# x's features on the partitions in another order: three weights loaded whole, and the places of the first and last groups searched anew

## Chip, cores and metric

The kernel runs on one core of a Trainium2 chip. The metric is device time in microseconds of one execution; the kernel before takes 2419.2 us, the median of three runs.

## What is computed

Two layers over 128 graphs of 128 nodes with 512 features, all in float32, with one mask `adj` for all graphs:

```python
# layer 0: attention, 8 heads of 64
q, k, v = x @ Wq + bq, x @ Wk + bk, x @ Wv + bv
attn = softmax(q_h k_h^T / 8 + (1 - adj) * -1e9)
x = layernorm(x + (attn v) @ Wo + bo)
# layer 1: graph attention
h = x @ W
e = leaky_relu(h a1 [i] + h a2 [j], 0.2) * adj
x = layernorm(x + elu(softmax(e) h + beta * h))
```

## The kernel before

**Groups.** The 128 graphs are done in 64 groups of two. The products of a group with a weight (512 x 512 against 512 x 256) are made of 2 x 2 blocks with seven products instead of eight: `product(name, g, n)` (L274) is the n-th of them. The sums of blocks that this needs are made once for each weight (`weight_sum`, L211: four steps, in place in part), and for each group's x (`block_sum`, L241, on GpSimd). The results come out of PSUM partly through ScalarE (`take_part`, L321) and partly through VectorE (`add_block`, L371), and a product that reuses a part of PSUM waits for the one that was read there.

**x with features on the partitions.** The products of q, k and v need x with its features on the partitions. `load_blocks` (L82) reads a group's x in four transfers, one for each quarter `a` of the features: partition `a*32 + r` gets the tokens `32 b + r`. `turn_x` (L233) then turns 32 x 32 blocks on VectorE, one instruction for each graph of the group, so that partition `a*32 + c` holds the features `a*128 + m*32 + c`, m = 0..3. Wq, Wk and Wv must have their rows in the same order, so `load_turned` (L102) reads each in four transfers to 32 partitions, four rows of 2 KB to a partition:

```python
queue(a, two).dma_start(
    out=t[a * Q : (a + 1) * Q],
    in_=src[a * P : (a + 1) * P].rearrange("(m c) f -> c m f", c=Q),
)
```

For Wq two of the four, and for the first x blocks two of the four, are issued from ScalarE, everything else of this from SyncE. Wo and W of layer 1 (`load_weight`, L128) are loaded with one transfer each to 128 partitions; biases, the mask, beta and the rows of a come through GpSimd's queue (`load_later`, L156).

**Order.** Nothing is left to a scheduler: `rows(g)` (L650) and `last_rows(g)` (L725) list the steps of a group with places, `other` (L792) replaces the places for the groups 0 to 3 and the last ones, and further steps (`weight_sum`, `wa_column`, `make_beta`, the loads) get places of their own. `lay` adds 37.33 per group, and the steps are issued sorted by place; so a place says only what stands ahead of what on each engine, and each engine works through its list in order, waiting where data are missing.

```python
for place, (_, fn, *args) in zip(places, own):
    at(g * STEP + place, fn, *args)
```

At the start TensorE multiplies the identity 20 times (`keep_busy`, L141) while the first loads run. In the last group the seven products of Wo and W give way to plain ones (`plain`, L351), whose weights are loaded a second time into the tiles of Wq and Wk (`load_again`, L131).

Of the kernel before, what the change touches and what calls it, by code (L numbers as in the profile page):

```python
# [13 lines left out]
P = 128  # L14
Q = 32
# [3 lines left out]
STEP = 37.33  # L19
# [3 lines left out]
def gnn_two_layers(  # L23
# [34 lines left out]
    nc = tc.nc  # L58
# [19 lines left out]

    def queue(a, two):
        return nc.scalar if two and a >= 2 else nc.sync  # L80

    def load_blocks(g):  # L82
        t = grp.tile([P, G, 4, P], F32, tag="xb", name=f"xblk_{g}", bufs=1)
        for a in range(4):
            queue(a, g == 0).dma_start(
                out=t[a * Q : (a + 1) * Q].rearrange("r t b d -> r (t b) d"),
                in_=x[g * G : (g + 1) * G, :, a * P : (a + 1) * P].rearrange(
                    "t (b r) d -> r (t b) d", r=Q
                ),
            )  # L90
        return t
# [10 lines left out]
    def load_turned(t, src, two=False):  # L102
        for a in range(4):
            queue(a, two).dma_start(
                out=t[a * Q : (a + 1) * Q],
                in_=src[a * P : (a + 1) * P].rearrange("(m c) f -> c m f", c=Q),
            )
# [14 lines left out]
    load_turned(wq_sb, wq, two=True)  # L122
# [110 lines left out]
    def turn_x(g, t):  # L233
        if t == 0:
            xT[g] = grp.tile([P, NC, G * N], F32, tag="xT", name=f"xT_{g}")
        nc.vector.transpose(
            xT[g][:, :, t * N : (t + 1) * N].rearrange("p m (b r) -> p b m r", r=Q),
            xblk[g][:, t].rearrange("p b (m c) -> p b m c", c=Q),
        )
# [485 lines left out]
    def last_rows(g):  # L725
        b0, b1 = g * G, g * G + 1
        return (
            (-61.75, fetch_blocks, g), (-45.225, turn_x, g, 0), (-43.975, turn_x, g, 1),
            (-41.605, block_sum, "x", g, 3), (-40.445, block_sum, "x", g, 1),
            (-39.705, block_sum, "x", g, 2), (-38.965, block_sum, "x", g, 4),  # L730
            (-27.57, product, "k", g, 1), (-25.805, product, "q", g, 7),
            (-24.91, product, "k", g, 7), (-23.25, take_part, "k", g, 1, 0, 0),
            (-23.145, product, "q", g, 1), (-21.38, product, "k", g, 6),
            (-18.97, take_part, "k", g, 6, 1, 0), (-18.31, take_part, "q", g, 1, 0, 0),
            (-17.675, fetch_x, b1), (-17.225, fetch_x, b0), (-14.395, product, "q", g, 6),
            (-13.085, take_part, "q", g, 6, 1, 0), (-12.825, residual, b0),
            (-12.63, product, "k", g, 2), (-11.545, residual, b1),
            (-11.515, add_block, "k", g, 0, 0, 2, 1), (-10.865, product, "q", g, 5),
            (-9.75, take_part, "q", g, 5, 1, 1), (-7.98, product, "k", g, 5),
            (-7.97, add_block, "q", g, 1, 1, 7, 5), (-6.865, take_part, "k", g, 5, 1, 1),  # L740
            (-6.215, product, "q", g, 2), (-6.02, add_block, "k", g, 1, 1, 7, 5),
            (-5.32, product, "k", g, 4), (-4.425, product, "k", g, 3),
            (-4.355, add_block, "q", g, 0, 0, 2, 1), (-3.31, take_block, "k", g, 0, 1),
            (-1.79, product, "q", g, 4), (-0.575, add_block, "q", g, 1, 0, 4, 6),
            (-0.155, add_block, "k", g, 1, 0, 4, 6), (-0.025, product, "q", g, 3),
            (1.09, take_block, "q", g, 0, 1), (1.97, scores, b0), (3.09, scores, b1),
            (3.56, mask, b0, 0), (3.99, product, "v", g, 1), (4.23, mask, b0, 1),
            (4.9, row_max, b0), (5.08, take_part, "v", g, 1, 0, 0), (6.12, mask, b1, 0),
            (6.26, exps, b0, 0), (6.6, product, "v", g, 6), (7.05, exps, b0, 1),
            (7.24, mask, b1, 1), (7.84, exps, b0, 2), (7.91, row_max, b1), (8.63, exps, b0, 3),  # L750
            (9.21, product, "v", g, 2), (9.42, exps, b1, 0), (9.56, row_inv, b0),
            (10.21, normalise, b0, 0), (10.81, normalise, b0, 1),
            (10.82, add_block, "v", g, 0, 0, 2, 1), (11.4, product, "v", g, 7),
            (11.41, normalise, b0, 2), (12.01, normalise, b0, 3), (12.61, exps, b1, 1),
            (12.75, attn_write, b0), (13.78, exps, b1, 2), (14.57, exps, b1, 3),
            (15.9, attn_read, b0), (16.55, row_inv, b1), (16.66, take_part, "v", g, 6, 1, 0),
            (17.04, normalise, b1, 0), (17.64, normalise, b1, 1), (17.83, product, "v", g, 5),
            (18.62, normalise, b1, 2), (19.22, take_part, "v", g, 5, 1, 1),
            (19.6, normalise, b1, 3), (19.74, add_block, "v", g, 1, 1, 7, 5),
            (19.75, product, "v", g, 3), (20.34, attn_write, b1), (20.58, turn_attn, b0, 0),  # L760
            (20.62, product, "v", g, 4), (21.24, turn_attn, b0, 1),
            (21.36, take_block, "v", g, 0, 1), (22.6, add_block, "v", g, 1, 0, 4, 6),
            (23.49, attn_read, b1), (24.37, attend, b0), (26.17, attend_evict, b0),
            (26.99, plain, "w", b0), (27.96, turn_attn, b1, 0), (28.62, turn_attn, b1, 1),
            (30.8, plain_take, b0), (30.89, attend, b1), (32.15, attend_evict, b1),
            (32.83, row_product, b0, 0), (33.56, row_product, b0, 1), (33.6, plain, "w", b1),
            (34.29, bn_stats, y, b0, "c"), (35.87, bn_aggr, b0, "c"),
            (36.07, add_eps, g, "c", 0), (37.3, plain_take, b1), (37.51, inv_std, g, "c", 0),
            (37.96, bn_stats, y, b1, "c"), (38.65, bn_aggr, b1, "c"),
            (38.85, add_eps, g, "c", 1), (39.02, scale_s, g, 0), (39.16, inv_std, g, "c", 1),  # L770
            (39.66, spread_s2, g, 0), (39.95, row_product, b1, 0), (40.68, row_product, b1, 1),
            (41.41, scale_s, g, 1), (41.58, edge, g, 0), (41.72, spread_s2, g, 1),
            (41.91, leaky, g, 0), (42.18, edge_max, g, 0), (42.45, norm_c, b0),
            (42.59, edge_exp, g, 0), (42.79, keep_busy, 6, "late"), (42.98, edge, g, 1),
            (43.31, leaky, g, 1), (43.58, edge_max, g, 1), (43.99, edge_exp, g, 1),
            (44.27, edge_inv, g, 0), (44.44, weights, g, 0), (44.77, edge_inv, g, 1),
            (44.94, weights, g, 1), (45.27, norm_c, b1), (45.83, turn_weights, g, 1),
            (46.03, turn_weights, g, 0), (46.25, weights_evict, g, 1),
            (46.55, weights_evict, g, 0), (46.69, aggregate, b1), (47.61, aggregate, b0),
            (48.34, aggregate_evict, b1), (48.93, aggregate_evict, b0), (49.07, plain, "h", b1),  # L780
            (52.52, plain, "h", b0), (53.85, elu_exp, b1), (55.81, elu_max, b1),
            (56.19, elu_exp, b0), (56.5, elu_sum, b1), (57.19, elu_max, b0),
            (57.88, elu_sum, b0), (58.57, bn_stats, u, b0, "f"), (59.26, bn_aggr, b0, "f"),
            (59.46, add_eps, g, "f", 0), (59.63, bn_stats, u, b1, "f"),
            (59.77, inv_std, g, "f", 0), (60.32, bn_aggr, b1, "f"), (60.52, add_eps, g, "f", 1),
            (60.69, shift, g, 0), (60.83, inv_std, g, "f", 1), (61.03, norm_f, b0),
            (61.71, shift, g, 1), (61.95, store, b0), (62.05, norm_f, b1), (62.97, store, b1),
        )
# [5 lines left out]
            1.72, 6.92, 7.58, 8.38, 15.14, 9.12, 15.88, 9.52, 11.53, 12.205, 10.415, 14.215,  # L794
            13.1, 17.525, 16.63, 18.64, 15.37, 11.31, 17.745, 13.995, 19.45, 16.52, 18.555,
            20.565, 15.79, 15.82, 21.365, 19.67, 21.375, 20.47, 20.48, 22.49, 21.595, 22.27,
            23.165, 24.28, 27.92, 24.7, 29.2, 25.825, 26.945, 27.18, 27.85, 14.89, 28.52, 15.76,
            16.85, 29.74, 29.88, 30.41, 33.58, 30.67, 31.46, 32.25, 17.37, 33.38, 33.72, 24.955,
            34.32, 28.715, 26.045, 35.73, 36.33, 34.94, 37.07, 36.93, 37.72, 27.845, 38.51,
            40.22, 28.935, 39.44, 40.62, 41.22, 34.8, 41.82, 42.42, 43.16, 46.31, 44.24, 44.9,  # L800
            50.26, 34.035, 43.68, 50.92, 35.8, 36.96, 46.57, 52.35, 48.57, 53.22, 54.23, 54.09,
# [194 lines left out]
```

## Time and profile before

| | |
|---|---|
| median of three runs | 2419.2 us (2416.99 to 2421.52) |
| the profiled execution | 2418.33 us, span 2416.6 us |
| granted TensorE clock, mean | 0.998 |
| busy share: TensorE, VectorE, ScalarE, GpSimd | 99%, 79%, 62%, 36% |
| data moved | 245.30 MB, 102 GB/s over the span |
| Wk: four transfers of 256 KB | 9.4 us from issue to landing, median |
| Wo: one transfer of 1024 KB | 7.6 us from issue to landing |
| first x blocks to use | VectorE starts to turn them at 5.17 us |

Spans and idle times are of one profiled execution, in microseconds from its start. A group of instructions is named by line, engine, operation and what it writes and reads. `pq`, `pk`, `pv` are PSUM tiles of the products for q, k, v (`eq`, `ev` the second ones), `tx` the block sums of x, `s_q`, `s_k`, `s_v` those of the weights, `psc` the scores, `po` the attention's output.

### The profile page before, as it was taken

Reading aid. Unit: us, or ns where it says so; the run is one execution under the profiler, and the core shown is the slowest. Engines: PE = TensorE matmul, PEld = TensorE weight load, DVE = VectorE, ACT = ScalarE, POOL = GpSimd, SP = SyncE. Lnnn points to the kernel's source line nnn. Section 1 sums busy time; section 2 is a strip of 40 time slices with the busy share of each in tenths; the row PEclk is TensorE's granted clock in tenths of the full one; section 3 lists DMA queues with packets and bytes.
Section 4 is the critical chain, followed back from the end, with each engine's and each line's share of the span. In section 5 each row is a group of like instructions: output and inputs, shape, how many; then the busy total and the mean of one; then the engine's idle time right before and its main releaser. Section 6 shows DMA issues by size and latency. Waiting matters only on the chain. (4 is left out here: it accounts for less than half of the span.)

```text
span 2416.6 us, 50056 instructions
## 1 busy us (share of the span) xinstructions
PE 2390.7 (99%) x17956; PEld 2206.0 (91%) x17956; DVE 1910.6 (79%) x4385; ACT 1487.9 (62%) x5310; POOL 860.6 (36%) x1045
## 2 busy tenths in 40 slices
PE   8999999999999999999999999999999999999998
PEld 7899999999999999999999999999999999999985
DVE  5777887788787877877877878778778787787787
ACT  3565666656656666566566566665665666656655
POOL 5332333324323333333233233332342333323332
PEclk9999999999999999999999999999999999999999
DMA  6323334334243243342342432423423324334331
GB/s 179 106 79 106 108 79 122 94 91 123 76 110 115 78 115 95 90 123 79 106 118 76 114 105 80 123 93 92 122 77 109 110 80 118 96 88 123 88 106 70
DMA packets 202633, 245.30 MB, mean 102 GB/s; under 512 B 18881, under 2 KB 149953, under 8 KB 202385
## 3 DMA queue, kind: packets, MB, share of 16 engines
q1 hardware_dynamic: 201152, 240.46, 34.7%
q8 instruction: 142, 2.33, 0.4%
q0 software_dynamic: 400, 0.86, 0.2%
q14 instruction: 107, 0.87, 0.1%
q10 hardware_dynamic: 832, 0.79, 0.1%
HBM read 141.37 MB, written 100.66 MB: 100 GB/s over the span
## 5 line engine op out<-in xcount | busy, mean ns | idle before, releaser
L411 ACT ACTIVATE s<-s,nmax 128x128 f32<-128x128 f32 x1024 | 397.7, 394 | 4.9 <-DVE nmax L405 4.8
L425 ACT ACTIVATE sb<-s,rinv 128x128 f32<-128x128 f32 x1024 | 327.0, 392 | 25.7 <-DVE rinv L418 20.3
L256 POOL TENSOR_TENSOR tw<-oT 128x256 f32<-128x256 f32 x63 | 46.2, 733 | 768.0 <-DVE oT L474 768.0
L445 POOL TENSOR_TENSOR x<-x,bo_b_in 128x512 f32<-128x512 f32 x128 | 164.3, 1294 | 362.4 <-DMA x<-in_x_dram 361.9
L317 ACT ACTIVATE part_q<-pq,bq_c 128x128 f32<-128x128 f32 x384 | 119.0, 361 | 239.0 <-PE pq L303 238.8
L411 ACT ACTIVATION_READ_ACCUMULATOR s<-s,nmax 128x1 f32 x1024 | 196.7, 192 | 0.0
L317 ACT ACTIVATE part_k<-pk,bk_c 128x128 f32<-128x128 f32 x384 | 120.2, 364 | 116.6 <-PE pk L303 69.4
L589 ACT COPY attT<-pat 128x256 f32<-128x256 f32 (+1 forms) x65 | 23.9, 369 | 263.0 <-PE pat L586 263.0
L397 DVE SCALAR_TENSOR_TENSOR s<-psc,amask 128x512 f32<-128x512 f32 x256 | 164.6, 683 | 25.7 <-PE psc L389 25.7
L454 DVE STREAM_TRANSPOSE attnT<-ab 128x512 f32<-128x512 f32 x256 | 178.8, 701 | 4.2 <-DMA ab<-scr 4.1
L514 DVE SCALAR_TENSOR_TENSOR ya<-w,wa_row 128x512 f32<-128x512 f32 x256 | 174.2, 681 | 4.4
L405 DVE TENSOR_REDUCE nmax<-s 128x8 f32<-128x1024 f32 x128 | 156.1, 1220 | 4.3
L327 DVE TENSOR_TENSOR part_w<-pw,x 128x256 f32<-128x256 f32 x189 | 80.0, 424 | 85.1 <-PE pw L297 85.0
L303 PE MATMUL pk<-xT,wk_sb 128*128 128x128 f32 x1024 | 139.8, 280 | 1.8 <-DMA wk_sb<-in_L_gnn_Wk_dram 1.8
L303 PE MATMUL pq<-xT,wq_sb 128*128 128x128 f32 x1024 | 135.1, 275 | 1.6 <-DMA wq_sb<-in_L_gnn_Wq_dram 1.4
L303 PEld LDWEIGHTS pq<-xT,wq_sb 128*128 128x128 f32 x1024 | 129.4, 192 | 5.5 <-issue 1.6
L303 PEld LDWEIGHTS pk<-xT,wk_sb 128*128 128x128 f32 x1024 | 129.0, 191 | 6.0 <-issue 1.9
L389 PE MATMUL psc<-kT,qT 64*128 64x128 f32 x2048 | 132.0, 279 | 0.0
L313 ACT COPY part_v<-pv 128x256 f32<-128x256 f32 x192 | 70.0, 365 | 100.3 <-PE pv L297 100.3
L389 PEld LDWEIGHTS psc<-kT,qT 64*128 64x128 f32 x2048 | 119.4, 188 | 11.7 <-issue 11.4
L464 PE MATMUL po<-attnT,v 128*64 128x128 f32 x2048 | 127.0, 276 | 1.3 <-DVE attnT L454 1.3
L599 PEld LDWEIGHTS pz<-attT,x 128*128 128x128 f32 x1024 | 124.3, 192 | 4.1 <-ACT attT L589 0.5
(681 smaller groups left out, 6544.0 us busy)
## 6 DMA issues: line engine op xcount, KB each, us to landing
scr<-sb SPq DMA_DIRECT2D x128, 512.0 KB, 2.7
ab<-scr SPq DMA_DIRECT2D x512, 128.0 KB, 3.1
x<-in_x_dram SPq DMA_DIRECT2D x128, 256.0 KB, 5.0
out_dram<-u SPq DMA_DIRECT2D x128, 256.0 KB, 2.1
xblk<-in_x_dram SPq DMA_DIRECT2D x254, 128.0 KB, 5.5
wk_sb<-in_L_gnn_Wk_dram SPq DMA_DIRECT2D x4, 256.0 KB, 9.4
wv_sb<-in_L_gnn_Wv_dram SPq DMA_DIRECT2D x4, 256.0 KB, 11.1
wo_sb<-in_L_gnn_Wo_dram SPq DMA_DIRECT2D x1, 1024.0 KB, 7.6
```

The lines of the kernel that those rows point to most:

```text
L303: nc.tensor.matmul(out[:, m * N : (m + 1) * N], a[:, c, m * P : (m + 1) * P], b[:, c, :], start=first and m == 0 and c == 0, stop=(c == 1) ...
L317: nc.scalar.activation(dst[:, m, :], src[:, m * N : (m + 1) * N], AF.Identity, bias=col)
L389: nc.tensor.matmul(psc[b][j][:, m, :], qT[g][feats, m, rows], kT[g][feats, m, rows], start=True, stop=True,)
L397: nc.vector.scalar_tensor_tensor(s_t[b][:, j * HP : (j + 1) * HP, :], psc[b][j], SCALE, amask.rearrange("p (o n) -> p o n", o=1).broadcast ...
L405: nc.vector.tensor_reduce(nmax[b], s_t[b], AX.X, ALU.max, negate=True)
L411: nc.scalar.activation(s_t[b][:, h, :], s_t[b][:, h, :], AF.Exp, bias=nmax[b][:, h : h + 1], accum_out=rsum[b][:, h : h + 1],)
L425: nc.scalar.mul(sb[b][:, :, h, :], s_t[b][:, h, :].rearrange("p (b c) -> p b c", c=Q), rinv[b][:, h : h + 1],)
L445: nc.gpsimd.tensor_tensor(xr[b], xr[b], later["bo"], ALU.add)
L454: nc.vector.transpose(attnT[b].rearrange("p h (a r) -> p a h r", r=Q)[:, rows], ab[b].rearrange("p a (h c) -> p a h c", c=Q)[:, rows],)
L464: nc.tensor.matmul(po[b][j * HD : (j + 1) * HD, m, :], vb[b][:, h * HD : (h + 1) * HD], attnT[b][:, j * HP + m, :], start=True, stop=True,)
L514: nc.vector.scalar_tensor_tensor(z, y[b], 1.0, wa_row[j], ALU.mult, ALU.mult, accum_out=s12[g][:, i, j : j + 1])
L599: nc.tensor.matmul(pz[b][:, c, :], x1[b][:, c * P : (c + 1) * P], attT[g][:, i, :], start=True, stop=True,)
```

## The change

The feature order is now `a*128 + 4 c + m` on partition `a*32 + c`. Four neighbouring rows of a weight then belong to one partition, and partition p has the rows 4p to 4p + 3, which lie together in memory (8 KB); each of Wq, Wk and Wv is one transfer to 128 partitions, from SyncE. `turn_x` reads the x blocks with a step of four elements. No other step changes what it does.

The places are new for the groups 0, 1 and 2, for the later part of group 3, for the last four groups and for the steps outside the groups. At the start of TensorE's list the order is now q1, q2, q7, v1, v2, q6, k1, k2, q5, k7, k6, q4, k5, q3, k3, k4, then k1 of group 1 and the scores of group 0; before it was q1, q2, q7, k1, k2, k7, v1, v2, k6, q6, k5, q5, k3, q3, q4, k4, q1 of group 1, v6, scores. SyncE now issues x of group 0 and W of layer 1 ahead of the x blocks of group 1, and Wo after them. On VectorE `make_beta` stands behind the first k add instead of behind the turn of group 1, and the first `wa_column` ahead of that turn. In the last group the two graphs change places in the second layer.

```diff
     def load_blocks(g):
...
-            queue(a, g == 0).dma_start(
+            (nc.scalar if g == 0 and a >= 2 else nc.sync).dma_start(
...
-    def load_turned(t, src, two=False):
-        for a in range(4):
-            queue(a, two).dma_start(
-                out=t[a * Q : (a + 1) * Q],
-                in_=src[a * P : (a + 1) * P].rearrange("(m c) f -> c m f", c=Q),
-            )
+    def load_turned(t, src):
+        nc.sync.dma_start(out=t, in_=src.rearrange("(p m) f -> p m f", m=NC))
...
-    load_turned(wq_sb, wq, two=True)
+    load_turned(wq_sb, wq)
...
-            xblk[g][:, t].rearrange("p b (m c) -> p b m c", c=Q),
+            xblk[g][:, t].rearrange("p b (c m) -> p b m c", c=Q),
...
-    at(16.62, load_later)
-    at(17.22, load_weight, wo_sb, wo)
-    at(19.82, load_weight, w1_sb, w1)
+    at(15.205, load_weight, w1_sb, w1)
+    at(15.265, load_later)
+    at(21.105, load_weight, wo_sb, wo)
...
-    at(20.89, make_beta)
+    at(19.425, make_beta)
...
-    at((NG - 1) * STEP + 1.09, load_again, wq_sb, wo)
-    at((NG - 1) * STEP + -3.31, load_again, wk_sb, w1)
+    at((NG - 1) * STEP + -0.726, load_again, wq_sb, wo)
+    at((NG - 1) * STEP + 1.074, load_again, wk_sb, w1)
```

The last store of the last group goes from place 62.97 to 61.979; the rest of the diff is numbers of this kind.

## The prediction

> **What bounds the kernel now.** I read the page first (shares of the engines, the 40 slices), then the waits of the tensor engine (PE) in the long middle, then its timeline and the windows at the start, the DMA issues, and last VectorE (DVE) around the step that the change touches.
>
> ```profile
> span 2416.6 us, 50056 instructions
> PE 2390.7 (99%) x17956; PEld 2206.0 (91%) x17956; DVE 1910.6 (79%) x4385; ACT 1487.9 (62%) x5310; POOL 860.6 (36%) x1045
> ```
>
> PE is busy 99% of the span. Its waits between 150 and 2290 us:
>
> ```profile
> PE pq L303 <- DVE qT L375: 2.1, 7, 0.4
> PE pq L303 <- ACT part_q L317: 0.2, 1, 0.2
> ```
>
> That is 2.3 us in 2140. In between, only less matmul work could help, and the change removes none; the built orders agree there: 2976 PE rows in a run are the same in both kernels. So the change acts on the first 40 us and on the last stretch. The timeline of PE at the start (start, length, in brackets the idle time before):
>
> ```profile
> 2.71 7.58 PE L145 MATMUL early<-ident 128*128 128x128 f32 x40 [2.71 <-POOL ident masks.py:199]
> 11.69 2.02 PE L303 MATMUL pq<-xT,wq_sb 128*128 128x128 f32 x16 [1.40 <-DMA wq_sb<-in_L_gnn_Wq_dram]
> 13.55 1.06 PE L303 MATMUL eq<-tx,s_q 128*128 128x128 f32 x8
> 16.36 2.02 PE L303 MATMUL pk<-xT,wk_sb 128*128 128x128 f32 x16 [1.75 <-DMA wk_sb<-in_L_gnn_Wk_dram]
> ...
> 23.57 3.75 PE L297 MATMUL pv<-wv_sb,xT 128*128 128x256 f32 x8 [4.29 <-DMA wv_sb<-in_L_gnn_Wv_dram]
> ...
> 36.33 1.03 PE L297 MATMUL pv<-s_v,tx 128*128 128x256 f32 x4
> ```
>
> Three waits, one for each weight: 1.40 + 1.75 + 4.29 = 7.44 us. The windows (length, busy of PE, PEld, DVE, ACT, POOL, granted clock, DMA share, GB/s) add a second price:
>
> ```profile
> 15.00:20.00 5.00, 2.92 (x24) 2.75 (x24) 3.55 (x7) 0.63 (x2) 0.00 (x0) 1.00 1.04 236
> 20.00:25.00 5.00, 1.43 (x4) 1.19 (x5) 0.01 (x1) 0.00 (x0) 1.32 (x2) 0.74 1.12 234
> 25.00:30.00 5.00, 5.00 (x23) 4.55 (x22) 1.64 (x3) 1.00 (x3) 4.32 (x4) 0.58 1.05 375
> ```
>
> The 4.29 us gap drops the clock to half; the first products after it run slow: v1 and v2 take 3.54 us (23.57 to 27.11), against 1.73 for such a pair later; the next two take 1.71 and 1.08 against 0.89. That is 2.8 us. And the DMA share is 1 throughout: the loads are limited by what the engines move, 235 GB/s while 32-partition pieces run, 375 when wo and w1 (128 partitions each) run.
>
> **The start, step by step.** Wq, Wk, Wv as one transfer each (1.05 MB). By 5.2 us 0.83 MB had moved, the first x blocks (0.52) among them. Up to the end of Wv remain 3 x 1.05 + 0.52 + 0.1 (mask, biases) - 0.83 = 2.94 MB. At 375 GB/s that takes 7.8 us: Wq at about 7.5, Wk 10.2, Wv 13.0. Here a rule stands against the row: the Trainium skill, "SBUF — State Buffer", section on the DMA port swizzle, gives 189 GB/s for partitions 0..31 and 328 for all 128 at 1 MiB, since 32 partitions reach half of the ports. This case's 235 and 375 lie above both, in the same proportion. By the rule's 328 Wv lands at 14.2; by the row at 13.0. I take the row and add half a microsecond for GpSimd's own loads (0.77 MB from 10.7 us on).
>
> PE cannot start before its warm-up matmuls end, at 2.71 + 7.58 = 10.29, and Wq is then there: of the 1.40 us wait all goes. Up to 36.33 PE did for group 0 q1+q2 (1.86 us), k1+k2 (1.79), v1+v2 (1.73), ten more products of q and k (0.895 each) and one of group 1: 15.2 us at full clock. The new order holds the same products ahead of the first scores, with v1+v2 third. So without waits it is through at 10.29 + 15.2 = 25.5 instead of 36.33: 10.8 us less (7.44 of waits, 2.8 of half clock, 0.6 of seams).
>
> What of it comes back as new waits? (a) v1 is reached at 10.3 + 1.86 + 0.9 = 13.05, Wv is there at 13.0 to 14.2: 0 to 1.1, I take 0.5. Gaps of 1.40 and 1.75 left the clock at 1.00, so no half clock. (b) The x blocks of group 1 are now issued behind x and w1, 2.1 MB more, with GpSimd's 0.77: 7.6 us at 375, 8.8 at 328, so about 21 to 23; DVE turns them behind the adds of group 0, at about 23, and PE wants them at 24.6: 0 to 2, I take 0.5. (c) beta_i, on DVE at 31.99 before, now stands behind the first k add. It waits for beta, which landed 7.8 us after its issue at 10.16, at 18.0. Behind it on DVE are the q adds; the product q4, which PE reaches at about 20, needs the add of q7 and q5. Slack 2 us: 0, at worst 3 to 4, I take 0.3. wa_column of w1 stands in the same queue, for the rows of a (landed at 19.6 and 20.6) and w1 (about 20): 0.2. Together 1.5 of 10.8 come back: **-9.3 us**. The softmax of group 0 follows 20.7 us behind its scores before (37.29 to 58.00), filled with other products, and 19.5 us of products stand there now: near zero, in the range. Fewer issues (7 on SyncE, 2 on ScalarE gone) lie beside the load and cost nothing.
>
> **The turned read.** turn_x reads its 32 elements with a step of 4 floats instead of side by side, 128 times:
>
> ```profile
> L236 DVE STREAM_TRANSPOSE xT<-xblk x128: 656/668/711, 5.2 to 2307.0; 128x512 f32<-128x512 f32 x128
> ```
>
> and the cover behind it, in DVE's timeline of one group of the middle:
>
> ```profile
> 773.05 0.20 DVE L418 RECIPROCAL rinv<-rsum 128x8 f32<-128x8 f32 x1 [2.23 <-ACT s L411]
> ```
>
> No row of the trace has such a read on DVE. The same page's rule ("SBUF — State Buffer", section on the specifications, cachelines) speaks against the change: lines are 16 bytes, full speed needs two hits on a line, and here each element takes a line of its own. It states no factor. Lower bound: nothing, 668 ns; below nothing is excluded[...]. Upper: twice, 1.3 us. I take 1.0 (between; the nearest row, that of the same instruction, is the lower end). At 1.0 DVE gets 2 x 0.33 us more per group, 42 us in all; by the row alone none. Either way PE sees nothing: behind the pair DVE idles 2.23 us waiting for ScalarE before the reciprocal, and the turned x is wanted by PE 7 us later (767.4 to 774.4). Without that cover each group would pay the 0.66. At the start the pair ends at 7.2 instead of 6.5, under the warm-up.
>
> **The last stretch.** The last four groups and the reload of Wq and Wk are only reordered. PE waits there for 0.80 + 0.20 + 0.43 + 0.56 us at 2316, 2337, 2340 and 2374; the last place drops from 62.97 to 61.98 (places are the kernel's own figures, an estimate at best). The reload stays ahead of the last writes of the attention, at 2345, 34 us before its use. From the first plain product on the chain is the same, with the two batches changed over. Between 0 and -2.0, or some tenths worse if a new wait comes; I take **-0.8**.
>
> Sum: -10.1. The profiled execution took 2418.33 (span 2416.6 and 1.7 around it), so 2408.2; it lay 0.9 under the median of 2419.2, so the median should be about **2409**.
>
> **Rivals.**
> - *The loads are no faster* (limited by memory, not by partitions). For it: the DMA share is 1 in both stretches. Against: 375 GB/s when wo and w1 run. At 235, Wv lands at 17.7; v1 waits 4.6 us, and half clock costs 2.8 again; with (b) later by as much as PE is, 3.4 of 10.8 stays: 2415.5. Chance 0.05.
> - *DVE's queue takes the place of the weights.* Beta and a come through GpSimd's queue, which took 8 to 10 us per load while it shared the engines with SyncE's 2 KB rows; beside rows of 8 KB its turns may come later still. Beta at 22 stops q4 for 3 us, and a at 24 delays the turn of group 1 by 2: 5 us come back: 2413.5. Chance 0.15.
> - *Better than the sum*: no new wait, and the old ones of the end gone: -10.8 - 2.0: 2406.5. Chance 0.17.
> - *Slower: the turned read is no cheap one.* It decides from 668 + 2230/2 = 1.8 us per transpose on: then the reciprocal, and with it the attention chain, is late in each of some 60 groups. At four times (2.67 us), 4.0 - 2.2 = 1.8 us per group, if passed on whole, is 107 us: 2516. For it: the rule; against: twice stays inside the cover. Chance 0.04.
> - That the change does not do what it says is excluded: the built queue holds three transfers of 128 x 2048.
>
> **Numbers.** The forecast's own case has 0.59. A difference under 0.2% (4.8 us) is about what a measurement of this kernel cannot tell from none. Faster by more: forecast, better, DVE's queue: 0.91; the loads' rival (3.7 us less) falls within: 0.05; slower 0.04. The range, 2405 to 2414, takes in the second and third rival and leaves out the other two and a tail.
>
> **What would show it.** Right: one issue each of wq, wk, wv, landing by 8, 10.5 and 13 to 14 us; PE's first real product at 10.3, no wait over 1.5 us before the first scores, these near 26 to 27 us; clock 1.00 throughout; middle waits as before; the transpose under 1.8 us. Wrong: a clock of 0.5 after 15 us, PE waits on DVE at 20 to 26 us, GB/s under 300 before 13 us, or new PE waits in every group.

## The result: half of what was forecast

After takes 2414.45 us (median of 20 runs, 2409.89 to 2418.57), before 2419.54 beside it (20 runs); the ratio is 0.9982, 95% interval 0.9975 to 0.9989. So it is faster, by 5.1 us between the medians (4.3 between the two profiled executions) where 10.1 was forecast, and 0.5 us above the range. Run twice more on other chips the same kernel came to 0.9976 and 0.9978. The profiled execution took 2414.03 us (span 2412.2). The ratios here are not quotients of the medians, and differ from them by up to 0.0005. Two of the 21 executions of the last run below, at 2729 and 3525 us with a mean granted clock of 0.947 and 0.654, are left out of its ratio.

The head of the page: PE as busy as before, VectorE (DVE) 47 us busier.

```profile
span 2412.2 us, 50040 instructions
PE 2387.4 (99%) x17956; PEld 2205.3 (91%) x17956; DVE 1957.7 (81%) x4385; ACT 1485.5 (62%) x5310; POOL 860.8 (36%) x1045
```

PE's timeline at the start (start, length, in brackets the idle time before):

```profile
9.99 2.02 PE L295 MATMUL pq<-xT,wq_sb 128*128 128x128 f32 x16 [0.79 <-DMA wq_sb<-in_L_gnn_Wq_dram]
11.85 1.06 PE L295 MATMUL eq<-tx,s_q 128*128 128x128 f32 x8
15.40 2.58 PE L289 MATMUL pv<-wv_sb,xT 128*128 128x256 f32 x8 [2.50 <-DMA wv_sb<-in_L_gnn_Wv_dram]
17.78 1.91 PE L295 MATMUL pq<-tx,s_q 128*128 128x128 f32 x8
19.49 2.23 PE L295 MATMUL pk<-xT,wk_sb 128*128 128x128 f32 x16
...
29.87 1.39 PE L381 MATMUL psc<-kT,qT 64*128 64x128 f32 x20
```

Of three waits two are short or gone, but one of 2.50 us for Wv is left, where 0.5 was allowed. The windows (length, busy of PE, PEld, DVE, ACT, POOL, granted clock, DMA share, GB/s):

```profile
5.00:10.00 5.00, 4.21 (x32) 4.05 (x31) 2.20 (x3) 0.98 (x1) 2.54 (x4) 1.00 0.93 277
10.00:15.00 5.00, 2.90 (x24) 2.71 (x24) 4.83 (x7) 0.93 (x3) 3.17 (x6) 1.00 1.02 391
15.00:20.00 5.00, 4.60 (x19) 4.19 (x20) 2.02 (x3) 0.64 (x3) 4.33 (x4) 0.67 1.04 371
```

The rate is 391 GB/s from 10 us on, as forecast, but 277 in the 5 us before. And 0.67 in the third row is a stretch of half clock, by the clock records from 16.67 to 20.08 us: 3.41 us, where before had 6.83. The five products behind the gap took 6.16 us (15.40 to 21.56).

**Where the time went.** I laid the two traces side by side, product by product. After is ahead by 6.5 us at the products just before the first scores, by 4.9 at 89 us, 3.7 at 120 us, 3.0 at 2159 us and 4.3 at the end. So the start brought less than forecast, and nearly half of it was gone again within four groups, where the forecast had "near zero". Between 30 and 125 us PE waits in after:

```profile
PE pq L295 <- DVE qT L367: 1.3, 1, 1.3
PE eq L295 <- DVE kT L367: 1.2, 1, 1.2
PE po L456 <- DVE attnT L446: 0.6, 1, 0.6
PE pk L295 <- DVE kT L367: 0.3, 1, 0.3
```

All four are for DVE, 3.4 us together (a "k sum" or "q sum" below is an `add_block` of k or q on DVE, here `kT` and `qT`). Before had 1.5 there, so these waits make 1.9 of the 2.8 us by which the lead fell (6.5 to 3.7). The last stretch was better than forecast in this execution, 1.3 us instead of 0.8, in spite of a new wait (PE's waits from 2290 us on):

```profile
PE eq L295 <- DVE kT L367: 1.7, 1, 1.7
```

### The profile page after: what moved, and what is told of

Read it like the earlier page. It is cut to its first block, busy times and chain, and to the rows that moved or that the text cites. A ratio compares the mean times of both kernels' runs of the same rounds, so it can differ in the third digit from the quotient of the medians.

```text
span 2412.2 us, 50040 instructions
## 1 busy us (share of the span) xinstructions
PE 2387.4 (99%) x17956; PEld 2205.3 (91%) x17956; DVE 1957.7 (81%) x4385; ACT 1485.5 (62%) x5310; POOL 860.8 (36%) x1045
## 4 chain that ended last, share of the span: by engine, by line
PE 92%; DVE 3%; DMA 2%; ACT 1%; SPq 1%; issue 1%; POOL 0%; ACTq 0%; DVEq 0%; POOLq 0%
PE pw L289 11%; PE ph L289 11%; PE pq L295 11%; PE pv L289 11%; PE pk L295 11%; PE eq L295 9%; PE psc L381 5%; PE po L456 5%; PE pz L591 5%; PE ev L289 4%; PE eh L289 4%; PE ew L289 4%; PE pat L578 1%; DMA wv_sb<-in_L_gnn_Wv_dram 1%; ACT sb L417 1%
## 5 line engine op out<-in xcount | busy, mean ns | idle before, releaser
L228 DVE STREAM_TRANSPOSE xT<-xblk 128x512 f32<-128x512 f32 x128 | 134.7, 1096 | 5.1 <-DMA xblk<-in_x_dram 5.1
```

## Experiments

My theory after the result: the loads make the gain; Wv, wanted third and loaded third, comes too late and lets the clock fall; later the longer turns (`turn_x`) and DVE's order take some of it back. Rivals: the new places make the gain; the row length, not the 128 partitions; the turn costs nothing. Each run below has its own runs of before on its chip, so ratios are compared, not times (before's median was 2419.4 to 2424.4 on the five chips).

### Which half of the change makes the gain

`e1_loads_only` has before's places with after's loads and turn, `e2_places_only` the reverse.

> The places of before, with the three transfers and the turned read of after. Theory (the loads carry the gain, the new places put Wv third and lose part of it again): Wq, Wk, Wv land at 9.9, 12.6 and 15.4 as in after; before's order reaches its first v product only at about 16, so no wait over 1 us, no half clock, first scores at 27 to 28 instead of 37.3, and a time of 2409 to 2412. Rival (the places carry the gain, the form of the loads does little): within 2 us of before, 2418 to 2421.

Measured: 2414.76 us, ratio 0.9978 (0.9970 to 0.9986).

> The places of after, with the twelve 32-partition transfers and the plain read of before. Theory: Wq, Wk, Wv land at about 11.5, 16.3 and 23.5 as in before, and the v products, now third, wait for Wv some 8 to 10 us; first scores at 40 or later, time 2420 to 2425, slower than before. Rival (the places carry the gain): 2413 to 2416 as after.

Measured: 2419.41 us, ratio 1.0005 (0.9997 to 1.0013); PE waited 8.23 us for Wv. So the loads alone bring all that the change brings, and the new places nothing that can be measured, with them or without. The second run was expected to be slower than before, at 2420 to 2425 us, and is not. The first missed its number too: Wv released PE at 18.2 instead of 15.4, after a gap of 1.33, PE then waited 1.88 us for a q sum on DVE, and the scores came at 31.3.

### Rows of 8 KB, or 128 partitions at once

```diff
-        nc.sync.dma_start(out=t, in_=src.rearrange("(p m) f -> p m f", m=NC))
+        for a in range(4):
+            nc.sync.dma_start(
+                out=t[a * Q : (a + 1) * Q],
+                in_=src[a * P : (a + 1) * P].rearrange("(p m) f -> p m f", m=NC),
+            )
```

> After, with each of the first three weights as four transfers of 32 partitions, rows of 8 KB as in after, all from SyncE. Theory (what made the loads faster is that all 128 partitions are written at once): GB/s from 5 to 20 us back near 235 to 290, Wq at 11 to 12.5, Wv at 18 to 22, gap at the first v product 4 to 8 us with half clock, scores at 34 or later, time 2417 to 2421. Rival (the 8 KB rows made them faster): Wq, Wk, Wv at 10, 12.6, 15.4, time 2413.5 to 2415.5.

Measured: 2419.79 us, ratio 1.0003 (0.9995 to 1.0011): the gain is gone. The windows of this kernel:

```profile
10.00:15.00 5.00, 3.59 (x22) 3.62 (x23) 2.77 (x4) 0.62 (x2) 3.22 (x6) 0.76 1.03 222
15.00:20.00 5.00, 0.80 (x4) 0.51 (x3) 2.91 (x5) 0.00 (x0) 0.00 (x0) 0.84 1.00 204
```

222 and 204 GB/s with the same 8 KB rows, against 391 from 10 to 15 us in after. A rival is that four issues in the place of one leave the DMA engines idle between them. The trace speaks against it: the DMA share is 1.03 and 1.00 here too, and a packet of 8 KB takes 596 ns (median, 10 to 15 us) where it takes 309 ns in after. So each packet is slower, and what differs is how many partitions are written at once. (The rule weighed in the prediction, the Trainium skill's "SBUF — State Buffer", section on the DMA port swizzle, holds in its proportion, 328 to 189 or 1.74; here it is 391 to 222, or 1.76. These two figures, for single transfers of 1 MiB, are too low for loads that follow one another in a queue; what the same table gives for very large transfers, about 218 and 436, is nearer.) The gap for Wv is 6.46 us, and the half clock behind it lasts 6.83.

### The gap for Wv, and the half clock

Three repairs, each one edit on after: Wv issued second; the first two v products behind the first of k; seven products of the identity in the gap.

```diff
-    load_turned(wk_sb, wk)
-    load_turned(wv_sb, wv)
+    load_turned(wv_sb, wv)
+    load_turned(wk_sb, wk)
```

> After, with Wv issued second and Wk third. Theory (the 2.50 us gap and the half clock behind it, 1.7 us, are what Wv's place as third in the queue costs): Wv lands at 12.6, Wk at 15.4, the first v product is reached at 12.9 and the first k product at 15.5; no wait over 0.5 us, clock 1.00, first scores at 25.7 to 27 instead of 29.87, time 3 to 4 us under after: 2410 to 2412. Rival (DVE's sums of Wk, which can start only at 15.4 instead of 12.6, become the bound): the first scores move by less than 1 us, time as after, 2413.5 to 2415.5.

Measured: 2413.77 us, ratio 0.9972 (0.9961 to 0.9984). The v products started at 13.2 without a wait and the clock stayed at 1.00, but the scores came at 28.8, not at 26: now PE waits 2.60 us at 22.2 for a k sum, as the rival said. In part both are right.

> After, with the two first v products of group 0 four products later on PE, behind the first of k; loads and their order as in after. Theory (the gap and the half clock come from wanting Wv before it can be there): v is reached at 16.3, Wv is there at 15.4; no wait over 0.7 us between 10 and 25 us, clock 1.00, scores at 25.5 to 26.5 instead of 29.87. Of these 3.5 to 4.5 us, by what the run with Wv issued second gave back behind its scores, some 1 to 3 stay: time 2411 to 2413. Rival (something else, DVE or GpSimd, sets the time of the first three groups): scores earlier, but the first scores of the third group at 83.5 to 84.5 as in after, and time 2413.5 to 2415.

Measured: 2411.52 us, ratio 0.9966 (0.9954 to 0.9979), on five runs. No wait for Wv, clock 1.00, yet the scores at 29.4, almost where they were. 0.8 us of this is Wq, which released PE at 10.78 in this execution. PE's timeline of this kernel shows what else came in the gap's place:

```profile
26.09 1.16 PE L295 MATMUL eq<-tx,wk_sb 128*128 128x128 f32 x8 [1.22 <-DVE kT L367]
28.34 1.16 PE L295 MATMUL pk<-xT,wk_sb 128*128 128x128 f32 x8 [1.09 <-DVE xT L228]
```

and DVE's timeline why:

```profile
23.88 1.81 DVE L175 SCALAR_TENSOR_TENSOR wa_t<-w_sb,uf_in 128x512 f32<-128x512 f32 x1 [1.31 <-DMA w_sb<-in_L_gnn_W_dram]
25.62 0.08 DVE L175 DVE_READ_ACCUMULATOR wa_t<-w_sb,uf_in 128x1 f32 x1
25.62 0.41 DVE L367 TENSOR_TENSOR kT<-eq,part_k 128x256 f32<-128x256 f32 x1
27.21 2.06 DVE L228 STREAM_TRANSPOSE xT<-xblk 128x512 f32<-128x512 f32 x2 [1.17 <-DMA xblk<-in_x_dram]
```

The k sum that PE wants stands behind a column sum (`wa_column`) that waits for w1, the weight W of layer 1; the turn of group 1 waits for its x blocks, which are queued behind w1. These are cases (b) and (c) of the prediction: hidden in after behind the gap for Wv, and there as soon as it goes.

> After, with seven products of the identity put into PE's queue ahead of the first v product, where the 2.50 us gap was. Theory (the half clock from 16.7 to 20.1 us follows from the gap): the seven take 1.4 to 2 us, the idle time left is under 1.2 us, the clock stays at 1.00, the first v pair takes 1.73 instead of 2.38 and the four products behind it 3.6 instead of 4.6, scores 1.2 to 1.8 us earlier, at 28.1 to 28.7; time 2412.5 to 2414. Rival (the clock falls for another reason, the load or the start): half clock at the same place, scores at 29.5 to 30.2, time 2414 to 2416.

Measured: 2412.92 us, ratio 0.9969 (0.9958 to 0.9981). The window from 15 to 20 us of this kernel:

```profile
15.00:20.00 5.00, 4.23 (x31) 3.83 (x30) 2.49 (x3) 1.00 (x3) 3.81 (x3) 1.00 1.04 364
```

The clock stays at 1.00, and the same five products take 4.51 us (16.01 to 20.52) instead of 6.16: the half clock costs 1.65 us and follows from the idle time. The scores gained only 0.6, since Wq landed 0.8 later in this execution.

### What slows the first microseconds of the load

The packets in the trace show 32 of 128 bytes between 6.1 and 9.3 us, the two bias columns of q and k; most took some 0.2 to 1.0 us beside the 8 KB packets, where those of the column for v later took 0.04 each. Together the 32 took 16.0 us, which is 1.0 us of each of the 16 DMA engines.

```diff
-    bq_c = column(bq, "bq_c")
+    bq_c = cpool.tile([P, NC], F32, tag="bq_c", name="bq_c")
+    nc.gpsimd.memset(bq_c, 0.0)
```

(and the same for `bk_c`)

> After, with the biases of q and k set to zero on the chip instead of loaded, so their part of the computation is left out. Theory (the 32 packets of 128 bytes of these two loads, which took about 0.6 us each between 6.1 and 9.3 us while the weights ran, hold up the weights): GB/s from 6 to 9 us rises from 218 to near 400, all three weights land 1.0 to 1.4 us earlier (Wv at 14.0 to 14.4), the gap falls to 1.2 to 1.5 us, no half clock, scores at 26.5 to 27.5, time 2410.5 to 2412.5. Rival (4 KB cannot hold up 3 MB; Wv is late for what is queued behind it, x and w1): Wv at 15.2 to 15.4 as in after, gap 2.3 to 2.5, time 2413.5 to 2415.5.

Measured: 2413.39 us, ratio 0.9973 (0.9963 to 0.9983). From 5 to 10 us:

```profile
5.00:10.00 5.00, 4.64 (x32) 4.48 (x31) 2.33 (x3) 0.00 (x0) 2.22 (x4) 1.00 0.98 365
```

365 instead of 277 GB/s; Wv comes 0.7 us earlier, the gap is 1.94, the clock does not fall there, scores at 28.0. Right in direction, half of the size expected. (The mask's 64 KB also went earlier in this run, so not all of the rate is due to the bias packets.)

### What gives the start's gain back

`e9_x_before_w1` mends what the repair with v behind k uncovered: x blocks of group 1 ahead of w1 and of x_0, x_1 (x of the groups 0 and 1 in its plain order), the first column sum behind the turn.

> The run with v behind k, and further: the x blocks of group 1 are issued ahead of w1, the plain rows x_0 and x_1 behind it, and the first column sum of w1 on DVE stands behind the turn of group 1. Theory (the 1.22 and 1.09 us that PE waited at 26 and 28 us, for a k sum behind DVE's wait for w1 and for the turn of group 1, come from the order of the issues): both fall under 0.4 us, first scores at 26 to 27.5 instead of 29.43, the first scores of the fourth group 1 to 2 us earlier than 121.58, time 1 to 2 us under that of the run with v behind k: 2409.5 to 2411.5. Rival (DVE and GpSimd bound the first three groups): the start is 2 us earlier, the fourth group within 0.7 of 121.6, time within 1 of the run before it.

> After itself once more, unchanged, to see how far its start is the same each time. Theory: Wq at 9.8 to 10.8, a gap of 2.3 to 2.8 us at the first v product and one stretch of half clock behind it; the waits for DVE at 50, 83, 116 and 2311 us as before, within 0.3 us; time 2413.5 to 2415.5. Rival (the gap is chance): no gap over 1 us, and 2411 to 2413.

Measured, on one chip: 2418.19 us, ratio 0.9974 (0.9964 to 0.9983), against 2418.51, ratio 0.9976 (0.9967 to 0.9985) for after itself. The scores came at 26.84, 2.9 us earlier than in after beside it, as forecast; but the fourth group was ahead by 0.5 only, and the time is the same. So the three microseconds were given back before 122 us. After itself did not repeat in all: the gap for Wv was 3.11 us, above the 2.3 to 2.8 expected, with 3.41 us of half clock behind it, and the wait of 1.31 us at 116 us did not come back.

`e11_no_row_sums` leaves out DVE's once-only work for the rows of w1 times a (13.6 us busy between 20 and 60 us in after).

> After, without the once-only work on DVE for the rows of w1 times a (eight column sums, two times centring): the two rows are set to zero, so the edge terms that depend on them are left out. Theory (the start's gain is given back between the scores and 122 us because DVE's once-only work, with the longer turns, makes k and q sums late): the waits at 50 and 116 us fall to under 0.5 us each, the stretch from the first scores to those of the fourth group is 90 to 91.2 us instead of 92.7, time 2412 to 2413.3. Rival (they are late for ScalarE or GpSimd): the stretch stays at 92.3 to 93, time 2413.8 to 2415.5.

Measured: 2414.56 us, ratio 0.9961 (0.9949 to 0.9973), on five runs, better than expected as a ratio; the stretch from the first scores to those of the fourth group is 90.1 us against 92.7 and 91.5. The window from 26 to 60 us shows it, first before:

```profile
26.00:60.00 34.00, 34.00 (x276) 32.13 (x275) 25.97 (x53) 21.18 (x81) 22.17 (x20) 0.95 0.48 146
```

then after,

```profile
26.00:60.00 34.00, 32.73 (x277) 29.63 (x276) 30.88 (x55) 19.50 (x77) 19.25 (x18) 1.00 0.32 101
```

the run with x ahead of w1,

```profile
26.00:60.00 34.00, 30.85 (x257) 27.21 (x257) 30.93 (x55) 18.46 (x75) 23.81 (x21) 1.00 0.31 98
```

and the run without the row sums:

```profile
26.00:60.00 34.00, 34.00 (x298) 31.18 (x297) 20.65 (x34) 21.15 (x84) 19.34 (x21) 1.00 0.33 106
```

The third and fifth numbers are the busy time of PE and DVE. When PE comes early to this stretch, DVE has 30.9 of 34 us to do and PE stands idle for 1.3, and for 3.2 when it comes earlier still. Without the once-only work PE is never idle there. The longer turn has its part in this: in the two profiles with x read side by side (next section) DVE is busy for 28.9 and 28.6 of the 34 us, PE is never idle there either, and the stretch is 91.6 and 90.4 us. So DVE's load in the first groups is the new bound of this stretch.

Moving only the end of the centring of the two rows (`wa_centre`), the last three steps, behind the first attention of group 0:

> After, with the three last steps of the once-only centring of the two rows moved on DVE from about 43 to 49 us behind the sums of q and k of group 1, to about 55; nothing is left out. Theory (these steps, with the longer turns beside them, make the k sum at 50 us late): the wait of 1.2 us at 50 us falls under 0.4, the stretch from the first scores to those of the fourth group is 90.0 to 91.2 us (92.7 and 91.5 in the two runs of after), time 1 to 2 us under after beside it. Rival (the work is only moved, and makes a wait of the same size further on): the stretch stays at 91.5 to 92.7, time within 0.7 of after.

> Both repairs: the first v products behind the first of k, and the centring moved back. If the gains add up: no gap over 0.7 us at the start but for Wq, no half clock, no wait over 0.5 us at 50 us, 3 to 5 us under after beside it. If a common bound stands behind both (DVE in the first three groups): 1 to 2.5 us under after.

> After itself, unchanged, for the comparison within this call: 5 to 6 us under before, gap at the first v product 2.3 to 3.2 us.

Measured, on one chip: 0.9976 (0.9968 to 0.9984), both repairs 0.9979 (0.9971 to 0.9986), after 0.9978 (0.9971 to 0.9985). The wait at 50 us went as expected (the stretch was 92.0 us against 93.0 in after beside it), but no gain can be told from the times: on this evidence the rival, that work only moved does not help, stands. Both repairs missed: no half clock was expected, and in this profile there were three stretches of 3.41 us, one at 27.09 us behind waits of 1.18 and 0.69 us for DVE, one at 85.12 behind a wait of 2.10 us, and one at 2317; from the first scores to those of the fourth group it took 94.9 us.

### The longer turn

`e5_plain_turn` and `e16_plain_turn_again` are one kernel: after with x read side by side, so that the features of x and the weights' rows do not match. After's own turn:

```profile
L228 DVE STREAM_TRANSPOSE xT<-xblk x128: 1062/1095/1141, 5.1 to 2307.1; 128x512 f32<-128x512 f32 x128
```

> After, with x read side by side (as before) in the turn, so that the features of x no longer match the rows of the first three weights: q, k and v are computed of a mixed-up order, with the same amount of work. Theory A (the longer turn, 1.09 instead of 0.66 us, is not wholly hidden: it stands ahead of the k and q sums in the new places of DVE's queue): the PE waits at 50 and 116 us (1.2 and 1.3 us) and the one at 2311 (1.7) shrink to under 0.6 each, and the time falls by 2 to 4 us to 2410.5 to 2412.5. Theory B (these waits come from the new places alone): waits and time as in after, 2413.5 to 2415.5, within 1 us.

> After with x read side by side, as in the earlier run of this name (q, k and v are of a mixed-up order of features). If the longer turn costs what single waits showed (1.2 at 50 us, some tenths at 116, 0.6 at 2311): 1.5 to 3 us under after beside it. If it costs nothing, as predicted: within 0.8 of after. If each of the 60 groups pays a little: 4 us or more under after, and fewer waits of PE for the q sum in the middle.

Measured: 2411.38 us, ratio 0.9963 (0.9949 to 0.9976) on five runs, and 2416.59, 0.9969 (0.9958 to 0.9980), the latter beside after at 0.9978. Each turn takes 668 ns again, as in before. The first ratio lies 3 to 5 us under those of after on other chips, the second 2 us under after beside it; the intervals overlap, so the size is not settled. Of the waits, the 1.2 us at 50 us is gone in both; the one at 116 stayed at 0.9 and 0.8, the one at 2311 at 1.1 and 1.7.

> After, with each turn of x done twice, into the same place. By the prediction's cover (2.23 us in which DVE waits before the reciprocal, of which the longer turn takes 0.86), the 2.2 us more per group pass 1.4 by 0.8 us, and nearly every group pays it: a period of 37.6 to 38.0 instead of 36.98, 2455 to 2480. Rival (the cover is larger, since DVE has other idle time that can be moved up to the turn): period 36.98 to 37.1, time 2414 to 2424.

Measured: 2527.56 us, ratio 1.0428 (1.0415 to 1.0442), far outside both. The waits of PE in the middle of this kernel:

```profile
PE ph L290 <- DVE h L368: 80.2, 56, 2.2
PE pq L296 <- DVE qT L368: 5.6, 18, 0.4
```

The period rose from 37.16 to 38.94 us (20 groups each), 1.78 us for 2.32 us more of turning (4.32 from the first turn to the next instruction, against 2.00 in after). So in after only about 0.5 us of cover is left behind the pair of turns; with the 0.83 that the pair grew by (1.18 in before), before had about 1.4, not 2.23. This takes all that goes beyond the cover as passed on to PE. DVE's timeline of one group of this kernel shows who was late:

```profile
1185.50 0.19 DVE L411 RECIPROCAL rinv<-rsum 128x8 f32<-128x8 f32 x1
1185.61 4.38 DVE L229 STREAM_TRANSPOSE xT<-xblk 128x512 f32<-128x512 f32 x4
1189.92 0.65 DVE L474 BATCH_NORM_STATS2 stats_f<-u 128x6 f32<-128x512 f32 x1
1190.49 0.40 DVE L368 TENSOR_TENSOR h<-ph,part_h 128x256 f32<-128x256 f32 x1
```

The idle time that I had counted as cover stands before the next reciprocal, at 1194 us; but ahead of it stands this sum of h, and PE, which wants the part of PSUM that it reads, waits for it: 1.40 us at 1191.

### The wait at 2311 us

In three of the profiles (four pieces, after the third time, both repairs) a wait of 1.9 to 2.0 us at this place was followed by 3.41 us of half clock at 2316 to 2320, and without the bias loads by the same at 2311. In after's first profile the wait was 1.75 and the clock stayed at 1.00. One k sum moved up seven places in DVE's queue:

```diff
+        if fn is add_block and args == ("k", NG - 2, 1, 1, 7, 5):
+            pieces[i] = (2310.6, k, fn, args)
```

> After, with one k sum of the last but one group moved seven places up in DVE's queue, ahead of the second turn of the last group; nothing else is moved. Theory (the new places put this sum too late, PE waits 1.7 to 2.0 us for it at 2311 us, and in some executions the clock falls for 3.41 us behind that wait, another 1.7): the wait falls under 0.4, no half clock at 2315 to 2325, the stretch from the first scores of the 60th group to the end is 211 to 211.8 us (212.8 in after, 214.0 in before, 214.7 where the clock fell), time 2 to 3 us under after, a ratio to before of 0.9965 to 0.9972. Rival (something else behind it takes the time, the wait only moves): stretch at 212.5 or more, ratio 0.9975 to 0.9985.

> The same, and the first v products behind the first of k. If the start's gain carries: 0.5 to 2 us under the run beside it, a ratio to before of 0.996 to 0.9967, the best of all. If it does not (DVE and GpSimd bound the first three groups): within 0.6 us of the run beside it.

Measured, on one chip: 2412.41 us, ratio 0.9976 (0.9966 to 0.9985), and 2413.87, 0.9975 (0.9968 to 0.9981). The wait fell to 1.0 (now for a q sum), the last stretch to 211.8 us from 212.8, the clock stayed at 1.00 there; the ratio is no better than after's, though the medians of this run and of before beside it (2419.35) would give 0.9971, so that a gain of some 2 us is not excluded. And with v behind k, the k sum at 26.9 waited 2.26 us, with 6.83 us of half clock behind it, and the medians give 0.9977. No run that leaves nothing out beats after by more than the intervals allow to tell.

## Why the forecast was wrong, step by step

- **Part that held.** One transfer to 128 partitions moves 391 GB/s from 10 us on (375 taken); the stretch with 32 partitions 235. The turned read lasts 1.095 us (1.0 taken). The new places do no measurable good by themselves.
- **(a) Wv: the first step that failed.** "The row" of 375 GB/s was applied to the whole 7.8 us. The first five ran at 277, Wq landed at 9.9 instead of 7.5 and Wv at 15.4 instead of 13.0. Without the bias columns (and with the mask earlier) the rate was 365; that is one cause, of 0.7 of the 2.4 us by which Wv is late. The rest was not tried alone. Two things more are visible in the packets: about 0.24 MB of x_0, x_1 and w1, queued behind Wv, had moved before Wv's last packet began at 14.26 (0.6 us at 391 GB/s), and PE started 0.8 us after that packet's end. The wait is 2.0 us larger than taken.
- **"Gaps of 1.40 and 1.75 left the clock at 1.00, so no half clock"**: right for such gaps, but this one was 2.50. It cost 1.65. Together: -6.5 at the first scores instead of -9.3 (2.0 and 1.65 more; 1.0 less, as the waits of (b) and (c) did not come; and 0.3 less, as the first product ran at 9.99 and not at 10.29: this makes -6.95, and 0.45 is not accounted for). The warm-up had no fixed end at 10.29: it ended at 9.20, as its matmuls are spaced 0.11 us from 6.46 us on, and 0.21 before; in before this step came at 8.79.
- **"Near zero" behind the scores: the second step that failed.** I had weighed the attention chain there, not DVE. DVE's load in that stretch is 31 of 34 us when PE is early, and 2.8 us were given back. In before, where PE came 6.5 us later, it waited there for DVE for 1.5 us only. This is a term that was put at nothing, and the largest miss beside (a).
- **(b), (c), and the rival "DVE's queue".** GpSimd's loads came sooner, not later (a in 5.9 us after its issue, before 8.9), and beta stopped nobody; the 2413.5 of this rival came near the time by another way. What (b) and (c) named came up as soon as the gap for Wv was taken away: the x blocks of group 1 landed at 24.7 to 26.7 us (21 to 23 forecast) and w1 at 24.1 (about 20).
- **The cover of the turn: mis-placed.** The point from which it decides was put at 1.8 us per turn; the run with doubled turns puts it near 1.4 (0.67 plus half of 1.4). At 1.095 the long middle keeps its period (36.98 us, the median, in both), but DVE's reserve is smaller by 0.83 us in each group, and two runs suggest that this costs some 2 to 4 us in all. 1.2 us of it is seen, as idle time of PE between 26 and 60 us; where the rest would lie is not shown.
- **Last stretch**: -1.3 in the profiled execution for -0.8; in others a fall of the clock behind the wait at 2311 takes about as much away again. In the profiled pair the sum is then -6.5 + 2.8 + 0.7 (the long middle, 120 to 2159 us) - 1.3 = -4.3 us.
- **Two slips of the sums, without weight.** 375 to 235 GB/s is 1.60, not "the same proportion" as the rule's 1.74. The loads' rival keeps 3.4 us of the gain, and 2419.2 - 3.4 is 2415.8, not 2415.5.

What stays open: why, for all the repairs at the start, medians stay within the interval of after's. In the run with x ahead of w1, 2.4 of the 2.9 us gained at the first scores were gone again by the fourth group, beside waits for DVE. But two things differ from profile to profile by as much as a repair brings: the waits of 0.15 to 0.6 us for q sums in the long middle (3 to 17 of them, 0.7 to 5.0 us together), and the stretches of half clock ahead of the end (0 to 3 in the runs of after and its repairs, 1.7 us each). With one profile of each kernel they cannot be told from its repair.

## What to carry to other kernels

Cost a load by the rate of the stretch in which it runs, its slow beginning included, and ask of each transfer whether its consumer's place in the order is later than its landing. When a stall at the start goes, look at the next engine's busy time in the stretch behind it: work that had been done in the shadow of the stall can then be in the way. Cover behind an instruction ends at the first thing in its queue that another engine waits for, not at the queue's next idle time.

## What was not expected of the hardware

- Half clock came in pieces of 3.41 us and multiples (3.41, 6.83, 10.24), and where a piece can begin is fixed within an execution. In the run with four pieces the stretches begin at 12.59, 19.42, 2320.00 and 2415.58 us (the last one after PE's work), which is 2.00, 674.0 and 28.0 steps of 3.4133 us apart; in all 14 profiles with more than one stretch the distances are whole numbers of such steps, to 0.01. So a trace can be cut into windows of this length, and what counts is how long PE idles within one. From 4.5 us to PE's last product the 20 profiles have some 14,000 windows at full clock. PE idled for 1.95 us or more in 18 of them, and half clock followed in the next window each time; of four windows with 1.87 to 1.93 us, two were followed by it; of all the others, with less, none was.
- So a wait of 2.50 us in after, of which 2.15 fell into one window, brought half clock, and one of 2.68 us, cut into 1.73 and 0.95 by the edge of a window, did not; the same holds for 2.60 us at 22 us (1.62 in one window). At 2311 us waits of up to 1.87 us never brought it, four of five from 1.91 to 2.00 us did, and the fifth, of 1.94, was cut in two by an edge. A wait of over 1.9 us is thus a risk, and chance decides only where it falls. The Trainium skill, "TensorE: Matmul & The Clock Gate", Part 1, tells of a free-running window of 3413 ns, and these steps confirm it. But it puts the idle time that it takes at a whole window, about 3.4 us, and here 1.95 us within one was enough.
- 32 packets of 128 bytes, 4 KB in all, held up transfers of 3 MB: 277 GB/s with them from 5 to 10 us, 365 without (and with the mask's 64 KB earlier).
- Reading 4-byte elements with a step of 16 bytes makes the same transpose 1.64 times as long (668 to 1095 ns).
